# A cross-attention block on one core: pair 0's probabilities through the exchange instead of TensorE, two exchange targets by turns, x of batch two loaded later, row sums repeated by ACT

## The chip, the cores and the metric

The kernel runs on one core of one Trainium2 chip. A core has TensorE (PE, with its weight loads as PEld), VectorE (DVE), ScalarE (ACT), GpSimd (POOL) and SyncE (SP), each working through its own instructions in order and waiting for the others by semaphores. Sixteen DMA engines move data; here nearly all transfers are issued by SP, in order. The metric is the time of one execution on the device in microseconds; less is better.

## The reference, cut to what matters

Four batches, 512 rows of x and 512 of the encoder each, width 512, 16 heads of 32, an MLP of 2048. All float32; the mask is all ones.

```
x = layer_norm(hidden_states, ln1_w, ln1_b)
q = (x @ q_w + q_b)            # heads of 32
k = (encoder @ k_w + k_b)
v = (encoder @ v_w + v_b)
scores = einsum('bhqd,bhkd->bhqk', q, k) / sqrt(32)
attn = softmax(where(mask, scores, min))
out = einsum('bhqk,bhkd->bhqd', attn, v) @ cproj_w + cproj_b
hidden = out + hidden_states
y = layer_norm(hidden, ln2_w, ln2_b)
y = gelu(y @ fc_w + fc_b) @ proj_w + proj_b
return hidden + y
```

## The kernel before

**Units.** The heads go in 16 groups w = 0 to 15, four heads of one batch each (batch w // 4). The 512 query rows of a group go in four tiles of 128, qt = 0 to 3. Unit u = 4w + qt is one (w, qt); two units of a group, qt = 0, 1 or 2, 3, make a half, and pair p = 2w + half numbers the halves from 0 to 31.

**One unit.** `scores` (L240 to L249): TensorE makes four score tiles of 128x512 into one PSUM tile `sc`, which is the only one, so that the next unit's scores wait until VectorE has read this one's. VectorE adds the mask and finds the row extreme (L245, one instruction and a short read for each head), ACT takes the exponential and adds up the rows (L249). `turn` (L277) then transposes each head's probabilities on VectorE in 32x32 blocks into `tb`. At the second unit of a pair it also makes the reciprocals of the row sums (L282), repeats each 32 times (`rr`, L284) and transposes that too (L285). `tb` has two buffers: a pair's transposes wait until the exchange of the pair two before it is through.

**The exchange.** 32x32 blocks transposed in place are not a transposed tile: the blocks must still change their places across partitions. `copies` (L319) does that by sixteen DMAs from SP, each from 32 partitions to 32 others, 136 KB each. Their target is `pT`, one buffer, for most pairs; `gt` for the pairs in `IN_G` = (2, 4, 6) (later the MLP's gelu results live there); `xe` for pairs 29 and 31. A pair that goes to `pT` is held back until the pair before it in `pT` has been used; `exchange` keeps that book (`waiting`, `held`).

**Pair 0** is the exception (`ON_PE`): `turn` transposes its 32 tiles of 128x128 on TensorE (`tpp`, L263), ACT and VectorE copy them out of PSUM (L268, L266), `over_sums` repeats the sums (L329) and `turn_sums` transposes them on TensorE (`tpr`, L337, L339). It has no exchange.

**Attend** (L362, L367): TensorE multiplies the transposed probabilities with the values `v`, VectorE scales with the repeated sums into `oT`. `AT` says at which unit pairs 1 to 6 are attended (pair 1 at u=7, 2 at 9, ..., 6 at 17); the others follow four units after their first unit, at even u. Attend stands ahead of the scores of its unit.

**What fills TensorE between.** `prep_k`, `prep_q`, `prep_v` make a group's k, q, v (`acck` L196, `accq` L206, `accv` L218; 3.5 to 3.8 us each), several groups ahead; each then loads the weights of the group two further on. `cproj` (`accc`, L399) follows a batch's last attend; LN2 and the MLP (`accf` L457, `accp` L467) of batches 0 and 1 fill the later groups. Batches 2 and 3 have their MLP at the end in seven half-size products (L561, L601). The results of all these go through one ring of four PSUM banks (`acc_tile`), each free again when VectorE or ACT has copied it out.

**Who sets the order.** Nothing is scheduled by a tool: the program order is written out, and each engine keeps it. `first[w]` and `later[w]` are lists of pieces of work with costs; `run` deals them out over the four units of a group, half a share before and half after the middle of each unit. `inputs(b)` gives four lists for batch b: x1 loads x, x2 is LN1 in three parts (statistics of two tiles, of two more with the reciprocal root on POOL, the normalisation), x3 transposes the result into `xT` (L137, L140, L142), x4 loads the encoder rows. `norm(0, ...)`, `stat(0, ...)` and `rs(0)` are LN2 of batch 0, `t2` its four transposes, `cb(0)` adds a bias on POOL.

Of the kernel before, what the change touches and what calls it, by code (L numbers as in the profile page):

```python
# [36 lines left out]
F32 = mybir.dt.float32  # L37
# [7 lines left out]
P = 128  # L45
B, L, D, H = 4, 512, 512, 16
HD = D // H
INNER = 4 * D
NT = L // P
ND = D // P  # L50
NG = ND
HG = H // NG
# [3 lines left out]
NI = P // HD  # L56
NW = B * NG
AHEAD = 3
NORMAL = 2
LAG = 4  # L60
IN_G = (2, 4, 6)
IN_XE = (29, 31)
AT = {7: 1, 9: 2, 11: 3, 13: 4, 15: 5, 17: 6}
ON_PE = (0,)
MW = 8
WARM = 9
PW = 2 * NT * HG * HD
# [7 lines left out]
def xattn_block(ctx: ExitStack, tc: tile.TileContext, x, encT, mask, q_w, k_w, v_w, c_w, fc_w, p_w, vecs, rows, out):  # L75
    nc = tc.nc
    scale = float(np.float32(1.0) / np.sqrt(HD).astype(np.float32))

    def pools(stack, **bufs):
        return [stack.enter_context(tc.tile_pool(name=n, bufs=k)) for n, k in bufs.items()]  # L80

    const, keep, hids, tiles, small = pools(ctx, const=1, keep=1, hids=6, tiles=4, small=4)
# [4 lines left out]
    one, two, kqp, five, six, fws = pools(att, one=1, two=2, kqp=4, five=5, six=6, fws=MW)  # L87
# [3 lines left out]
    ident = const.tile([P, P], F32, tag="ident", name="ident")  # L91
# [13 lines left out]
    S = {}  # L105
    Q = [nc.sync]

    def acc_tile(name):
        return ps_acc.tile([P, D], F32, tag="acc", name=name)
# [143 lines left out]
    def turn(w, qt):  # L253

        half, q = divmod(qt, 2)
        if 2 * w + half in ON_PE:
            if q == 0:

                S["pT", w, half] = two.tile([P, 2, NT, HG, P], F32, tag="tb", name=f"pT_{w}_{half}")
            for h in range(HG):  # L260
                tp = acc_tile(f"tpp_{w}_{qt}_{h}")
                for t in range(NT):
                    nc.tensor.transpose(tp[:, ts(t, P)], S["ps", w, qt][h][:, ts(t, P)], ident)  # L263
                o = S["pT", w, half][:, q, :, h, :]
                if h % 2:
                    nc.vector.tensor_copy(o, tp.rearrange("p (t q) -> p t q", t=NT))  # L266
                else:
                    nc.scalar.copy(o, tp.rearrange("p (t q) -> p t q", t=NT))  # L268
            return
        if q == 0:  # L270


            S["tb", w, half] = two.tile([P, NI, PW + 2 * HD], F32, tag="tb", name=f"tb_{w}_{half}")
        tb = S["tb", w, half]
        tv = tb[:, :, :PW].rearrange("p j (a t h q) -> p a h t j q", a=2, t=NT, h=HG)
        for h in range(HG):
            nc.vector.transpose(tv[:, q, h], S["ps", w, qt][h])  # L277
        if q == 0:
            return

        rs = small.tile([P, 2, HG], F32, tag="rsum", name=f"rsum_{w}_{half}")
        nc.vector.reciprocal(rs, S["sums", w][:, 2 * half : 2 * half + 2, :])  # L282
        rr = one.tile([P, 2, HG, HD], F32, tag="rr", name=f"rr_{w}_{half}")
        nc.vector.tensor_copy(rr, rs[:, :, :, None].broadcast_to([P, 2, HG, HD]))  # L284
        nc.vector.transpose(  # L285
            tb[:, :, PW:].rearrange("p j (a q) -> p a j q", a=2), rr.rearrange("p a h d -> p (a h d)")
        )
        waiting.append((w, half))
        if w < NW - 1 or half == 0:
            exchange()  # L290
# [3 lines left out]
    def exchange():  # L294

        while waiting:
            w, half = waiting[0]
            if 2 * w + half not in IN_G + IN_XE:
                if held:
# [5 lines left out]
    def copies(w, half):  # L305
        tb = S["tb", w, half]

        pair = 2 * w + half
        if pair in IN_G or pair in IN_XE:
            pT = (gt if pair in IN_G else xe).rearrange("p (i n) -> p i n", i=NI)  # L310
        else:
# [7 lines left out]
                q.dma_start(out=pT[ts(j, HD), i], in_=tb[ts(i, HD), j])  # L319
        S["pT", w, half] = pT  # L320

    def over_sums(w, half):

        if 2 * w + half not in ON_PE:
            return
        rs = small.tile([P, 2, HG], F32, tag="rsum", name=f"rsum_{w}_{half}")
        nc.vector.reciprocal(rs, S["sums", w][:, 2 * half : 2 * half + 2, :])
        rr = one.tile([P, 2, HG, HD], F32, tag="rr", name=f"rr_{w}_{half}")
        nc.vector.tensor_copy(rr, rs[:, :, :, None].broadcast_to([P, 2, HG, HD]))  # L329
        S["rr", w, half] = rr.rearrange("p a h d -> p (a h d)")  # L330

    def turn_sums(w, half):
        if 2 * w + half not in ON_PE:
            return
        tp = acc_tile(f"tpr_{w}_{half}")
        for q in range(2):
            nc.tensor.transpose(tp[:, ts(q, P)], S["rr", w, half][:, ts(q, P)], ident)  # L337
        rb = one.tile([P, 2 * P], F32, tag="rb", name=f"rb_{w}_{half}")
        nc.scalar.copy(rb, tp[:, : 2 * P])  # L339
        S["rb", w, half] = rb  # L340

    def attend(w, half):

        b, g = divmod(w, NG)
        if g == 0 and half == 0:
            S["oT", b] = one.tile([P, NG, L], F32, tag="oT", name=f"oT_{b}")
        v, pT = S["v", w], S["pT", w, half]
        on_pe = 2 * w + half in ON_PE
        av = acc_tile(f"av_{w}_{half}")
        o = S["oT", b][:, g, ts(half, 2 * P)]  # L350
        if on_pe:
            shape, kw = "p (a q) -> p a q", dict(a=2)
            p = [[pT[:, :, t, h, :] for h in range(HG)] for t in range(NT)]
            r = S["rb", w, half].rearrange(shape, **kw)
        else:
            shape, kw = "p (a i q) -> p a i q", dict(a=2, i=NI)
            pv = pT[:, :, :PW].rearrange("p i (a t h q) -> p t h a i q", a=2, t=NT, h=HG)
            p = [[pv[:, t, h] for h in range(HG)] for t in range(NT)]
            r = pT[:, :, PW:].rearrange("p i (a q) -> p a i q", a=2)
        for t in range(NT):  # L360
            for h in range(HG):
                nc.tensor.matmul(  # L362
                    av[ts(h, HD), : 2 * P].rearrange(shape, **kw), v[:, t, ts(h, HD)], p[t][h],
                    start=(t == 0), stop=(t == NT - 1),
                )
        o, a = o.rearrange(shape, **kw), av[:, : 2 * P].rearrange(shape, **kw)
        nc.vector.tensor_tensor(o, a, r, ALU.mult)  # L367
        if (w, half) in held:
            held.remove((w, half))
        exchange()  # L370
# [326 lines left out]
    def do(fn):  # L697
        return [(0.0, fn)]
# [66 lines left out]
    x1, x2, x3, x4 = inputs(1)  # L765
# [7 lines left out]
    first = [[] for _ in range(NW)]  # L773
    later = [[] for _ in range(NW)]
# [11 lines left out]
    def some(n):  # L786
        taken, mlp[:n] = mlp[:n], []
        return taken
# [7 lines left out]
    def cb(b):  # L796
        return do(lambda: c_bias(b))

    def pb_(b):
        return do(lambda: proj_bias(b))  # L800

    def rs(b):
        return do(lambda: ln_rs((2, b)))

    def stat(b, *ts_):
        return do(lambda: [stat2(b, t) for t in ts_])

    def norm(b, *ts_):
        return do(lambda: [norm2(b, t) for t in ts_])


    x1, x2, x3, x4 = inputs(2)
    first[3] = x1 + first[3] + cb(0)
    k, q, v = A(7)
    c, t2 = C(0), turns2(0)
    first[4] = [k] + x2[:1] + [q] + x2[1:2] + [v] + x4 + x2[2:]
    later[4] = c[:1] + x3[:2] + c[1:2] + x3[2:] + c[2:] + stat(0, 0, 1, 2, 3) + rs(0)
    k, q, v = A(8)
    first[5] = norm(0, 0, 1, 2, 3) + [q, k] + t2[:3] + [v] + t2[3:] + pb_(0) + some(5)
    k, q, v = A(9)  # L820
    x1, x2, x3, x4 = inputs(3)
    first[6] = [k, q] + some(5) + [v] + x1
    k, q, v = A(10)
    first[7] = [k, q] + x2[:1] + some(3) + x2[1:2] + some(3) + [v]

    k, q, v = A(11)
    first[8] = h_(1, 0, 1) + x2[2:] + [k, q] + x3[:2] + some(1) + x3[2:] + [v] + h_(1, 2, 3) + x4
    later[8] = cb(1) + C(1)
    k, q, v = A(12)
    first[9] = [q] + some(2) + [k] + some(3) + [v]  # L830
    k, q, v = A(13)
    first[10] = [k, q] + some(5) + [v]
    k, q, v = A(14)
    t2 = turns2(1)
# [3 lines left out]
    k, q, v = A(15)  # L838
# [6 lines left out]
    for w in range(NW):  # L845
        if w and w % NG == 0:
            make_mb(w // NG)
        work, rest = first[w], later[w]
        share = sum(c for c, _ in work + rest) / NT
        due = 0.0  # L850
        for qt in range(NT):
            u = w * NT + qt
            pair = AT.get(u, (u - LAG) // 2 if u >= LAG and u % 2 == 0 else None)
            if pair in AT.values() and u not in AT:
                pair = None
            if pair is not None:
                turn_sums(*divmod(pair, 2))
                attend(*divmod(pair, 2))
            scores(w, qt)
            on_pe = u // 2 in ON_PE  # L860
            if not on_pe:
                turn(w, qt)

            if qt == 2:
                work, rest = work + rest, []
            due += share / 2
            due -= run(work, due)
            if on_pe:
                turn(w, qt)
                if u % 2 == 1:  # L870
                    over_sums(w, qt // 2)
            due += share / 2
            due -= run(work, due)
        run(work + rest)
# [1 line left out]

    load_h(B - 1, *range(NT))
    run(some(2))
    turn_sums(NW - 1, 0)
    attend(NW - 1, 0)  # L880
    run(some(2))
    load_wa(0)
    run(some(2))
    turn_sums(NW - 1, 1)
    attend(NW - 1, 1)
    run(some(2))
    load_wa(1)
# [50 lines left out]
```

## Time and profile before

| | us |
|---|---|
| three runs | 825.77, 826.09, 826.44 |
| median of them | 826.09 |
| the profiled execution | 823.17 |
| its span, first to last instruction | 821.4 |
| TensorE busy | 805.0 |
| VectorE busy | 562.7 |
| ACT busy | 347.7 |
| POOL busy | 90.4 |
| exponentials on ACT (L249), 256 of 710 ns | 181.6 |
| block transposes on VectorE (L277), 248 of 690 ns | 161.6 |
| repeats of the sums on VectorE (L284), 31 of 414 ns | 12.8 |
| SP's waits for an attend's last step (L319 for L367), before 260 us | 25.3 |

The span is the part of an execution that the trace covers; all times in the trace count from its start. An engine's busy time is the sum over its instructions with overlaps counted once. Durations that a row gives for one instruction overlap with the next by some tens of ns: 690 ns for a transpose, but four of them start 0.60 us apart. In rows of waits the name behind the arrow is what ended the wait. The granted clock is TensorE's, as a share of full speed.

### The profile page before, as it was taken

What the parts mean: (1) busy time and instruction counts of PE and PEld (TensorE: products, weight loads), DVE (VectorE), ACT (ScalarE), POOL (GpSimd) and SP (SyncE); (2) the same over time, 40 slices, a digit from 0 to 9 for tenths busy, and PEclk for the clock granted to TensorE, in tenths of its full rate; (3) what the DMA queues carried; (4) which work ended last, traced back from release to release, by engine and by line L of the source; (5) the groups of instructions that cost most, each with busy time, mean ns of one, the idle gap of its engine ahead of it and who ended that gap; (6) DMA issues with size and microseconds to landing.
All of it is one profiled execution on the core that took longest, in us unless ns stands there. A gap on an engine that the chain in (4) does not pass through costs nothing.

```text
span 821.4 us, 11900 instructions
## 1 busy us (share of the span) xinstructions
PE 805.0 (98%) x4020; PEld 467.0 (57%) x4020; DVE 562.7 (69%) x1264; ACT 347.7 (42%) x741; POOL 90.4 (11%) x98
## 2 busy tenths in 40 slices
PE   9998999999999999999999999999999999999998
PEld 6553545454454554454544444434447888888887
DVE  3598989886576778667886667787426986268511
ACT  2455555346554744365435367556201331023200
POOL 1110003112000111000111210010201012200011
PEclk9998999999999999999999999999999999999999
DMA  9639998856668768677676676777734550023001
GB/s 327 231 88 237 239 247 233 218 147 161 173 164 222 183 166 237 162 209 194 159 212 179 157 197 159 199 181 174 211 116 162 193 171 14 26 77 89 2 13 39
DMA packets 59740, 134.91 MB, mean 164 GB/s; under 512 B 12144, under 2 KB 14320, under 8 KB 59552
## 3 DMA queue, kind: packets, MB, share of 16 engines
q1 hardware_dynamic: 58416, 130.73, 58.8%
q0 software_dynamic: 736, 2.29, 0.8%
q10 hardware_dynamic: 528, 1.14, 0.5%
q8 instruction: 32, 0.52, 0.3%
q14 instruction: 28, 0.23, 0.1%
HBM read 58.74 MB, written 6.29 MB: 79 GB/s over the span
## 4 chain that ended last, share of the span: by engine, by line
PE 85%; DMA 5%; DVE 5%; SPq 3%; issue 1%; ACT 1%; DVEq 0%; ACTq 0%
PE accp L467 14%; PE accf L457 14%; PE q L561 12%; PE sc L240 7%; PE accc L399 7%; PE av L362 6%; PE accv L218 4%; PE acck L196 4%; PE accq L206 4%; SPq L319 3%; PE q4p L601 2%; PE q3p L601 2%; PE q7p L601 2%; PE q2p L601 2%; PE q5p L601 2%; PE q6p L601 2%
## 5 line engine op out<-in xcount | busy, mean ns | idle before, releaser
L249 ACT ACTIVATE s<-s,mn 128x512 f32<-128x512 f32 x256 | 181.6, 710 | 138.0 <-DVE mn L245 137.8
L245 DVE CUSTOM_DVE_ANT_0 s<-sc,mb 128x512 f32<-128x512 f32 x256 | 161.3, 686 | 55.4 <-PE sc L240 55.2
L277 DVE STREAM_TRANSPOSE tb<-s 128x512 f32<-128x512 f32 x248 | 161.6, 690 | 9.5 <-ACT s L249 8.5
L457 PE MATMUL accf<-yT,fcw 128*128 128x512 f32 x256 | 115.5, 599 | 0.5 <-ACT v L223 0.3
L467 PE MATMUL accp<-pw,gt 128*128 128x512 f32 x256 | 115.0, 598 | 0.0
L457 PEld LDWEIGHTS accf<-yT,fcw 128*128 128x128 f32 x256 | 47.2, 190 | 65.5 <-issue 55.5
L467 PEld LDWEIGHTS accp<-pw,gt 128*128 128x128 f32 x256 | 47.2, 190 | 63.8 <-issue 61.1
L240 PE MATMUL sc<-kT,qT 32*128 32x512 f32 x512 | 73.8, 646 | 1.1 <-ACT qT L209 0.8
L218 PEld LDWEIGHTS accv<-wv,xe 128*128 128x128 f32 x512 | 58.8, 192 | 9.9 <-issue 6.2
L218 PE MATMUL accv<-wv,xe 128*128 128x128 f32 x512 | 60.7, 277 | 1.7 <-ACT xe L142 0.9
L362 PE MATMUL av<-pT,v 128*32 128x256 f32 x864 | 53.9, 391 | 6.7 <-DMA pT<-tb 6.7
L561 PE MATMUL q<-ys,gt 128*128 128x256 f32 x256 | 60.1, 379 | 0.0
L196 PE MATMUL acck<-xe,wk 128*128 128x512 f32 x128 | 59.6, 609 | 0.0
L206 PE MATMUL accq<-xe,wq 128*128 128x512 f32 x128 | 58.5, 599 | 0.0
L399 PE MATMUL accc<-wc,oT 128*128 128x512 f32 x128 | 56.9, 597 | 0.0
L561 PEld LDWEIGHTS q<-ys,gt 128*128 128x128 f32 x256 | 48.6, 190 | 6.6
L249 ACT ACT_TABLE_LOAD x22 | 28.2, 1283 | 52.7 <-DVE mn L245 52.7
L230 POOL TENSOR_TENSOR v<-v,row 128x512 f32<-128x512 f32 x16 | 20.3, 1269 | 261.5 <-ACT v L223 261.4
L249 ACT ACTIVATION_READ_ACCUMULATOR s<-s,mn 128x1 f32 x256 | 47.7, 187 | 0.0
L362 PEld LDWEIGHTS av<-pT,v 128*32 128x32 f32 x864 | 26.1, 112 | 36.7 <-issue 18.9
L561 PE MATMUL q<-yT,gt 128*128 128x256 f32 x192 | 46.3, 379 | 0.0
L367 DVE TENSOR_TENSOR oT<-av,pT 128x256 f32<-128x256 f32 x26 | 11.0, 422 | 46.7 <-PE av L362 43.9
(117 smaller groups left out, 855.2 us busy)
## 6 DMA issues: line engine op xcount, KB each, us to landing
pT<-tb SPq DMA_DIRECT2D x416, 136.0 KB, 2.4
fcw<-fc_w_dram SPq DMA_DIRECT2D x32, 256.0 KB, 3.4
pw<-p_w_dram SPq DMA_DIRECT2D x32, 256.0 KB, 3.5
gt<-fc_w_dram SPq DMA_DIRECT2D x32, 256.0 KB, 3.0
gt<-tb SPq DMA_DIRECT2D x48, 136.0 KB, 2.8
wk<-k_w_dram SPq DMA_DIRECT2D x16, 256.0 KB, 3.5
xe<-encT_dram SPq DMA_DIRECT2D x16, 256.0 KB, 6.0
wv<-v_w_dram SPq DMA_DIRECT2D x16, 256.0 KB, 3.1
```

The lines of the kernel that those rows point to most:

```text
L196: nc.tensor.matmul(acc, S["wk", w][:, d, :], eT[:, d, :], start=(d == 0), stop=(d == ND - 1))
L218: nc.tensor.matmul(acc[:, ts(t, P)], eT[:, d, ts(t, P)], S["wv", w][:, d, :], start=(d == 0), stop=(d == ND - 1),)
L240: nc.tensor.matmul(sc[:, h, :], qT[r, ts(qt, P)], kT[r, :], start=True, stop=True)
L245: nc.vector.tensor_tensor_reduce(out=s, in0=sc[:, h, :], in1=S["mb", w // NG], scale=1.0, scalar=FMAX, op0=ALU.add, op1=ALU.min, accum_out=mn,
L249: nc.scalar.activation(s, s, AF.Exp, bias=mn, scale=-1.0, accum_out=sums[:, qt, h : h + 1])
L277: nc.vector.transpose(tv[:, q, h], S["ps", w, qt][h])
L362: nc.tensor.matmul(av[ts(h, HD), : 2 * P].rearrange(shape, **kw), v[:, t, ts(h, HD)], p[t][h], start=(t == 0), stop=(t == NT - 1),)
L399: nc.tensor.matmul(acc, S["oT", b][:, g, ts(t, P)], wc[:, g, :], start=(g == 0), stop=(g == NG - 1))
L457: nc.tensor.matmul(acc, S["fcw", b, f][:, d, :], S["yT", b][:, d, :], start=(d == 0), stop=(d == ND - 1))
L467: nc.tensor.matmul(acc, gT[q % 2][:, k, ts(t, P)], S["pw", b, q * FQ + k], start=(k == 0), stop=(k == FQ - 1))
L561: nc.tensor.matmul(o, a[:, k], y[:, k], start=(k == 0), stop=(k == 1))
L601: nc.tensor.matmul(o[:, t], a[:, c, ts(t, P)], w[:, c], start=(c == 0), stop=(c == NP - 1))
```

## The change

It has four parts, all in how the work is ordered and on which engine it stands.

1. Pair 0 is treated as the others: its eight score tiles are transposed by VectorE and go through an exchange, and it is attended at u=5 in place of u=4. `ON_PE`, `over_sums` and `turn_sums` go.
2. `IN_G` becomes (1, 3, 5, 7): in batch zero `pT` and `gt` take the pairs by turns.
3. x of batch two is loaded by the first piece of w=4 (it was the first of w=3), behind the exchanges of batch zero; its statistics and normalisation move among the `cproj` pieces of w=4, its transposes to w=5, and the order of the pieces of w=5 changes with them.
4. In `turn`, for every pair, `rr` is made by ACT. At the second unit of a pair VectorE transposes three heads, then takes the reciprocals, then transposes the fourth head while ACT repeats the sums.

```diff
-IN_G = (2, 4, 6)
+IN_G = (1, 3, 5, 7)
 IN_XE = (29, 31)
-AT = {7: 1, 9: 2, 11: 3, 13: 4, 15: 5, 17: 6}
-ON_PE = (0,)
+AT = {5: 0, 7: 1, 9: 2, 11: 3, 13: 4, 15: 5, 17: 6}
...
     def turn(w, qt):
         half, q = divmod(qt, 2)
-        if 2 * w + half in ON_PE:
-            if q == 0:
-                S["pT", w, half] = two.tile([P, 2, NT, HG, P], F32, tag="tb", name=f"pT_{w}_{half}")
-            for h in range(HG):
-                tp = acc_tile(f"tpp_{w}_{qt}_{h}")
-                for t in range(NT):
-                    nc.tensor.transpose(tp[:, ts(t, P)], S["ps", w, qt][h][:, ts(t, P)], ident)
-                o = S["pT", w, half][:, q, :, h, :]
-                if h % 2:
-                    nc.vector.tensor_copy(o, tp.rearrange("p (t q) -> p t q", t=NT))
-                else:
-                    nc.scalar.copy(o, tp.rearrange("p (t q) -> p t q", t=NT))
-            return
...
-        for h in range(HG):
+        for h in range(HG - q):
             nc.vector.transpose(tv[:, q, h], S["ps", w, qt][h])
         if q == 0:
             return
         rs = small.tile([P, 2, HG], F32, tag="rsum", name=f"rsum_{w}_{half}")
         nc.vector.reciprocal(rs, S["sums", w][:, 2 * half : 2 * half + 2, :])
         rr = one.tile([P, 2, HG, HD], F32, tag="rr", name=f"rr_{w}_{half}")
-        nc.vector.tensor_copy(rr, rs[:, :, :, None].broadcast_to([P, 2, HG, HD]))
+        nc.scalar.copy(rr, rs[:, :, :, None].broadcast_to([P, 2, HG, HD]))
+        nc.vector.transpose(tv[:, q, HG - 1], S["ps", w, qt][HG - 1])
         nc.vector.transpose(
             tb[:, :, PW:].rearrange("p j (a q) -> p a j q", a=2), rr.rearrange("p a h d -> p (a h d)")
         )
...
     x1, x2, x3, x4 = inputs(2)
-    first[3] = x1 + first[3] + cb(0)
+    first[3] += cb(0)
     k, q, v = A(7)
     c, t2 = C(0), turns2(0)
-    first[4] = [k] + x2[:1] + [q] + x2[1:2] + [v] + x4 + x2[2:]
-    later[4] = c[:1] + x3[:2] + c[1:2] + x3[2:] + c[2:] + stat(0, 0, 1, 2, 3) + rs(0)
+    first[4] = x1 + [k, q, v] + x4
+    later[4] = c[:1] + x2[:1] + c[1:2] + x2[1:2] + c[2:3] + x2[2:] + c[3:] + stat(0, 0, 1, 2, 3) + rs(0)
     k, q, v = A(8)
-    first[5] = norm(0, 0, 1, 2, 3) + [q, k] + t2[:3] + [v] + t2[3:] + pb_(0) + some(5)
+    first[5] = x3[:2] + [k] + x3[2:] + norm(0, 0, 1, 2, 3) + [v] + t2[:2] + [q] + t2[2:] + pb_(0) + some(5)
...
```

In the order that results, the instructions of each engine differ in these places: TensorE loses the 34 transposes of pair 0, attends it behind the values chain of w=3, and has the transposes of x of batch two (`tp_2_0` to `tp_2_3`) among `acck` and `accv` of w=8; on SP exchange 0 stands ahead of wq of w=3 and wk of w=4 and w=5, x of batch two behind exchange 7, and exchange 8 ahead of the encoder rows of batch two; on POOL a value bias of w=7 stands ahead of the reciprocal root of batch two's LN1; on ACT every pair's second unit has the repeat behind its exponentials.

## The prediction

> **What bounds the kernel now.** I write u = 4w + qt for the unit of scores (w, qt), pair p for units 2p and 2p+1, and "exchange p" for the sixteen copies of pair p. The page's first part comes first: it says which engine is the bound.
>
> ```profile
> PE 805.0 (98%) x4020; PEld 467.0 (57%) x4020; DVE 562.7 (69%) x1264; ACT 347.7 (42%) x741; POOL 90.4 (11%) x98
> ```
>
> TensorE idles 16 us in all, so time comes from those idles, from work taken off it, or from waits added. Next, busy time by stage, with borders at the events below: stretch, length, busy time of PE, PEld, DVE, ACT, POOL, granted clock, DMA share, GB/s.
>
> ```profile
> 20.00:42.00 22.00, 20.55 (x110) 11.78 (x109) 11.51 (x31) 10.43 (x24) 4.49 (x5) 1.00 0.62 229
> 42.00:54.70 12.70, 12.70 (x102) 7.90 (x102) 12.56 (x32) 7.17 (x19) 1.27 (x1) 1.00 0.11 36
> 54.70:82.40 27.70, 23.55 (x124) 11.09 (x123) 24.92 (x66) 16.79 (x44) 1.27 (x1) 0.88 0.88 225
> 82.40:141.90 59.50, 59.50 (x420) 32.71 (x420) 55.30 (x134) 33.60 (x86) 9.48 (x8) 1.00 0.92 240
> 141.90:190.30 48.40, 44.14 (x258) 21.98 (x257) 38.98 (x91) 19.06 (x43) 9.85 (x10) 1.00 0.65 169
> 190.30:821.40 631.10, 625.89 (x2932) 368.13 (x2928) 412.46 (x899) 256.01 (x522) 62.08 (x64) 1.00 0.56 149
> ```
>
> The DMA engines stand almost idle from 42 to 54.7 (0.11) and are then full to 142; VectorE has 0.14 us of slack in 42 to 54.7. So early on PE's 100% hides a chain VectorE -> exchange -> attend. The order of time on TensorE (start, length, work, idle before it) shows where that surfaces:
>
> ```profile
> 27.58 1.91 PE L263 MATMUL tpp<-ident,s 128*128 128x128 f32 x16
> 34.02 1.89 PE L263 MATMUL tpp<-ident,s 128*128 128x128 f32 x12
> 36.54 0.66 PE L263 MATMUL tpp<-ident,s 128*128 128x128 f32 x4 [0.62 <-ACT qT L209]
> 50.08 0.38 PE L337 MATMUL tpr<-ident,rr 128*128 128x128 f32 x2
> ...
> 66.78 3.64 PE L362 MATMUL av<-pT,v 128*32 128x256 f32 x32 [3.34 <-DMA pT<-tb]
> 82.39 1.93 PE L362 MATMUL av<-gt,v 128*32 128x256 f32 x32 [0.45 <-DMA gt<-tb]
> 145.31 1.93 PE L362 MATMUL av<-pT,v 128*32 128x256 f32 x32 [3.40 <-DMA pT<-tb]
> ```
>
> and SP's queue what the exchanges stand behind:
>
> ```profile
> 54.68 10.12 SPq L319 DMA_DIRECT2D pT<-tb  x16
> 68.22 12.27 SPq L319 DMA_DIRECT2D gt<-tb  x16
> ...
> 115.28 1.87 SPq L155 DMA_DIRECT2D xn<-x_dram  x4
> 117.73 13.28 SPq L319 DMA_DIRECT2D gt<-tb  x16
> 132.72 10.29 SPq L319 DMA_DIRECT2D pT<-tb  x16
> ```
>
> An exchange costs SP 10.1 us and lands 2.4 us later (median of L319); right behind 1 to 1.5 MB of loads it takes 12.3 to 13.3.
>
> **Step 1, transposes off TensorE.** Next start less start, 1.84 + 3.01 + 0.32 = 5.2 us of PE go (the 0.62 wait included). That is not the gain: PE then waits for attend 1, so the path is VectorE's. Its order: x of batch one lands at 30.60 (both kernels), then stats to 32.24. New chain: scores of u=1 2.45 (four starts 0.61 apart) -> 34.7; three transposes at 0.60 -> 36.5; reciprocal 0.2; last transpose 0.6; transpose of the sums 0.4 -> 37.7; two stats 1.6; u=2 scores and transposes 2.45 + 2.41 -> 44.2; four norms 1.8 -> 46.0; u=3 2.45 + 1.8 + 0.2 + 0.6 + 0.4 -> 51.4. Before, pair 1 was ready at 54.6, because VectorE waited for tpp (2.1 + 0.5 + 1.3) and for scores behind them (1.9). So exchange 1 can start 3.2 us sooner although VectorE transposes eight tiles more.
>
> **Step 2, the added exchange.** Exchange 0: 37.8 to 47.9, landed 50.3; attend 0 at u=5 needs it at about 53 (sc of u=4 at 48.4 waits for VectorE, then a values chain, 3.7). Hidden by the idle queue; without that cover it would cost its 10 us. But wq, wk and wk (three 256 KB loads, issued at 34 and 41 to 46 before) now stand behind it and ahead of exchange 1. They delay it by 0 (drained by 51.4) to 3.3 us (0.79 MB at 240 GB/s); they go out from 48 on, so I take 0.5. Exchange 1 starts 2.8 us sooner. From it to attend 2 SP's order is unchanged, so attend 2 starts at 82.4 - 2.8 = 79.6. PE idles about 2 us at u=4, 3.6 before attend 1 and 2 to 3 before attend 2; these contain the removed work.
>
> The row first: after the 3.34 us idle the clock was 0.50 from 66 to 72 us, after the 3.40 us idle at 142 it stayed 1.00. The Trainium skill, "TensorE: Matmul & The Clock Gate" (section "Why this matters for your kernels"), warns of idles above about 3 us between bursts; the second idle shows that one need not halve the clock. By the rule attend 1 and the next scores would again take 3.64 and 1.96 instead of 1.93 and 1.14, 2.5 us more; by the row 0 or 2.5. Either way they end before exchange 2 lands, so the sum doesn't move.
>
> **Step 3, buffers by turns, x moved.** Pairs 1, 3, 5, 7 take gt and 0, 2, 4, 6 pT: the same alternation with the parity swapped, nothing by itself, except that pair 7 leaves pT free for pair 8. From 82.4 to 141.9 PE ran without a wait; the same instructions, from 79.6, end at 139.1. Exchange 6 no longer stands behind x: 117.7 - 2.8 - 2.0 = 113.0, plus 10.3, plus 1.6 for three weights -> 124.9. Pair 7 is ready at 126 (u=15's scores 2.8 sooner, and a repeat of 0.82 us less on VectorE): 126 + 10.1 + 2.4 = 138.5, under 139.1. The 3.40 wait goes; attend 7 starts at 139.1 instead of 145.3: **6.2 us ahead**. Margin 0.6.
>
> **Step 4, what x meets behind.** x's four loads (1.9 us of SP, some 5.4 to land) now stand ahead of wk, wq and exchange 8; they land near 144, wanted near 147. Encoder rows of batch two are moved behind exchange 8: issued 152 to 154, landed at 159.5, wanted at 161. What does cost is VectorE: from sc of u=18 (3 us after attend 7) it has u=18 4.9, u=19 5.4, four h adds 2.4, x's stats 3.2 and norms 1.9, LN2 stats 3.2, oT 0.4, so u=20's scores begin 24.4 us after attend 7, though PE offers them at 20. ACT's xe copy of tp_2_0 stands behind u=20's exponentials, kT behind that; tp_2_3 and the values chain need their two banks and wait 2.5 to 3. Counted by PE's pieces, the first accf begins 43.0 us after attend 7. Before: 190.3 (end of sc u=22) - 145.3, less accf 0's 3.6, = 41.4, including waits of 1.6. So **1.6 us is given back** (bounds: 1.6 gained if nothing waits, 4 lost if ACT and VectorE miss each other once more).
>
> **Step 5, sums repeated by ACT.** 31 copies (414 ns mean, 293 undisturbed) leave VectorE. No row has this copy on ACT; bounds are 0.29 (VectorE's own) and 1.30 (its longest); I take 0.36, ACT's copy of 128x256 at L339. The last transpose (0.60) covers it; at 1.30 each pair would be ready 0.7 us later. But ACT now waits for the reciprocal with its evictions queued behind: at 371.5 scores end, three transposes and reciprocal end near 373.5, ACT was free at 372.7, so 1.1 us later; with a table load behind, 0.55. After 190 nothing waits on VectorE, so its gain is nothing; ACT's delay is hidden by the four banks (accf ends at 354.2, its gelu at 357.8, its bank is next wanted after three more chains, near 364). PE waited for ACT only twice there, 0.87 each; 0 to 1, I take 0.2.
>
> **Sum.** 6.2 - 1.6 - 0.2 = 4.4 us. The profiled execution took 823.17 (span 821.4 and 1.8 around it), so 818.8; the shown runs have median 826.09, 2.9 above, and I carry the difference over: **821.7**.
>
> A rule that speaks against the change is in the Trainium skill, "VectorE: DVE Perf Modes" (section "Rules for kernel authors"): a 128x128 transpose goes to TensorE where its result may land in PSUM. By the rule, moving these off TensorE buys an exchange of 10 us for nothing, and the sum would be 831.7; by the row of stage 42.00:54.70 (DMA share 0.11) that exchange runs in an empty queue and costs 0, which is what I take.
>
> **Rivals.**
> - *Larger gain.* No wait in step 4, exchange 1 undelayed: 6.7 + 1.6 = 8.3, 817.8. For it: those 2.5 us hang on one ACT order; against it: VectorE's sum. Chance 0.20.
> - *Nothing comes of it.* The three loads delay exchange 1 by 3.3 rather than 0.5 and pair 7's margin is lost: 4.4 - 2.8 - 1 is about 0.6, 825.5. Speaks for it: 12.3 us of exchange 2 behind loads. Against: 3.5 us between their issue and pair 1's readiness. 0.13.
> - *Slower: ACT's wait reaches PE.* 24 pairs after 190 us, 0.55 to 1.1 each, some 20 us on ACT, with the gelu and value copies behind. From 30% of it on PE (6 us) the change is slower; at 45%, 9 us, the time is 830.7. For it: every odd unit has it, and PE there has 100% to lose. Against: six us of bank slack at 357. 0.21.
> - *The forecast*, 819.5 to 824.4: 0.46.
>
> Measurements of this kernel can't tell less than about 0.2% (1.65 us) from no change. Faster: 0.46 + 0.20 = 0.66; same 0.13; slower 0.21. The range of 8 in 10 leaves 0.05 below 818.0 and 0.14 of the slower case above 828.0.
>
> **What would show it.** Step 1: reciprocal of pair 1 near 50.3. Step 2: exchange 1 issued near 52, PE waiting there and before attend 2 near 79.6. Step 3: no wait at attend 7, near 139. Step 4: a wait of 2 to 3 us before the values chain of w=8 near 165. Step 5: PE as full after 190 as before. I am wrong if exchange 1 starts after 54, or if ACT waits appear on PE past 190 us.

## The result, and the profile after

| | before | after |
|---|---|---|
| median, us | 825.77 (824.24 to 826.44, five runs) | 820.96 (818.40 to 823.18, five runs) |
| profiled execution, us | 823.17 | 818.40 |
| its span, us | 821.4 | 816.6 |
| its mean granted clock | 0.996 | 0.998 |

The ratio is 0.9944, with an interval of [0.9921, 0.9966]: 4.8 us faster, both in the medians and in the two profiled executions. The first part of the page of after (busy time, share of the span, instructions):

```profile
PE 798.2 (98%) x3986; PEld 462.9 (57%) x3986; DVE 546.8 (67%) x1237; ACT 354.6 (43%) x766; POOL 90.5 (11%) x98
```

TensorE is busy 6.8 us less (mostly the 34 transposes, and some time at a halved clock) with the same share of the span, so it idles 18 us, 2 more than before. Busy time of after by stage, with borders at its own events (exchange 1 issued, attend 2, attend 7, first `accf`); columns as before:

```profile
50.67:78.83 28.16, 24.10 (x153) 11.49 (x153) 24.07 (x64) 18.35 (x47) 2.55 (x2) 0.94 0.90 231
...
138.86:182.41 43.55, 39.93 (x249) 20.30 (x248) 38.35 (x92) 18.14 (x44) 9.88 (x10) 1.00 0.69 186
182.41:816.60 634.19, 629.16 (x2940) 369.61 (x2936) 402.19 (x878) 263.13 (x543) 62.21 (x64) 1.00 0.56 149
```

The stretch from exchange 1 to attend 2 takes 28.2 us as it did before (27.7): it has moved as a whole, and TensorE still has 4 us of idle in it. The order of time on TensorE in after (start, length, work, idle before it):

```profile
47.98 1.14 PE L239 MATMUL sc<-kT,qT 32*128 32x512 f32 x8 [1.82 <-DVE mn L244]
...
62.97 2.55 PE L322 MATMUL av<-gt,v 128*32 128x256 f32 x32 [2.44 <-DMA gt<-tb]
65.45 2.09 PE L239 MATMUL sc<-kT,qT 32*128 32x512 f32 x8
...
78.83 1.93 PE L322 MATMUL av<-pT,v 128*32 128x256 f32 x32 [1.62 <-DMA pT<-tb]
...
138.86 1.93 PE L322 MATMUL av<-gt,v 128*32 128x256 f32 x32
...
167.75 0.65 PE L136 MATMUL tp<-ident,xn 128*128 128x128 f32 x4 [2.86 <-ACT xe L141]
```

Attend 7 (138.86) has no wait ahead of it; the wait of 2.86 us at 167.75 is new. SP's queue in after:

```profile
37.22 10.10 SPq L305 DMA_DIRECT2D pT<-tb  x16
50.67 10.33 SPq L305 DMA_DIRECT2D gt<-tb  x16
...
64.12 12.80 SPq L305 DMA_DIRECT2D pT<-tb  x16
...
113.15 10.06 SPq L305 DMA_DIRECT2D pT<-tb  x16
125.82 10.26 SPq L305 DMA_DIRECT2D gt<-tb  x16
136.76 1.87 SPq L154 DMA_DIRECT2D xn<-x_dram  x4
```

Exchange 0 stands in the stretch where the queue was idle. Exchange 1 goes out 4.0 us sooner than before (0.5 of it because everything in this execution is that much earlier: the first scores of the kernel begin at 22.30 and 22.83). x of batch two now follows exchange 7, and exchange 6 takes 10.06 us instead of the 13.28 it took behind x.

The account at the events, after against before: attend 2 3.6 us sooner, attend 7 6.45 sooner. From attend 7 to the values chain that waits 0.87 us for an `xe` copy (299.57 before, 295.12 after), 2.0 are given back. From there to the end of the span after takes 521.5 and before 521.8: 0.3 are gained. 6.45 - 2.0 + 0.3 = 4.8. This account is that of two executions, and both are 2.6 us faster than the median of their kernel. A second profiled execution of the changed kernel (10 below) has attend 7 5.6 sooner, 3.6 given back, 1.7 of them at a halved clock, and the same 0.3: 2.3 in all. The 4.8 of the result rests on the medians.

### The profile page after: what moved, and what is told of

The parts are those of the page before. It is cut to its first block, busy times and chain, and to the rows that moved or that the text cites. A ratio compares the mean times of both kernels' runs of the same rounds, so it can differ in the third digit from the quotient of the medians.

```text
span 816.6 us, 11880 instructions
## 1 busy us (share of the span) xinstructions
PE 798.2 (98%) x3986; PEld 462.9 (57%) x3986; DVE 546.8 (67%) x1237; ACT 354.6 (43%) x766; POOL 90.5 (11%) x98
## 4 chain that ended last, share of the span: by engine, by line
PE 84%; DVE 7%; DMA 5%; SPq 2%; ACT 1%; issue 1%; DVEq 0%; ACTq 0%
PE accf L417 14%; PE accp L427 13%; PE q L521 12%; PE sc L239 7%; PE av L322 7%; PE accv L217 5%; PE accc L359 5%; PE accq L205 4%; PE acck L195 4%; DVE s L244 3%; DVE tb L262 2%; SPq L305 2%; DMA xn<-x_dram 2%; PE q4p L561 2%; PE q3p L561 2%; PE q7p L561 2%
## 5 line engine op out<-in xcount | busy, mean ns | idle before, releaser
L262 DVE STREAM_TRANSPOSE tb<-s 128x512 f32<-128x512 f32 x224 | 146.3, 691 | 12.3 <-ACT s L248 9.5
L521 PEld LDWEIGHTS q<-ys,gt 128*128 128x128 f32 x256 | 48.6, 190 | 6.6
L322 PE MATMUL av<-pT,v 128*32 128x256 f32 x832 | 50.3, 382 | 2.1 <-DMA pT<-tb 1.6
L525 ACT ACTIVATE ga<-uc,vec 128x256 f32<-128x256 f32 x32 | 16.3, 508 | 60.1 <-DVE uc L493 60.1
```

Of the source, the lines that this page charges most:

```text
L322: nc.tensor.matmul(av[ts(h, HD), : 2 * P].rearrange(shape, **kw), v[:, t, ts(h, HD)], p[t][h], start=(t == 0), stop=(t == NT - 1),)
L521: nc.tensor.matmul(o, a[:, k], y[:, k], start=(k == 0), stop=(k == 1))
```

## The experiments

Twelve runs follow. Ratios are to the kernel before, run beside them on the same chip. The starts are those of the profiled executions. The first scores, ahead of which the kernels are alike, begin anywhere from 21.89 to 22.98 us, so that half a microsecond in a start says nothing.

| kernel | exchange 1 | attend 2 | attend 7 | wait ahead of it | span | median | ratio [95%] |
|---|---|---|---|---|---|---|---|
| before | 54.68 | 82.39 | 145.31 | 3.40 | 821.4 | 825.77 | |
| after | 50.67 | 78.83 | 138.86 | 0 | 816.6 | 820.96 | 0.9944 [0.9921, 0.9966] |
| 1 idle transposes added | 52.10 | 79.25 | 139.74 | 0.64 | 817.5 | 821.51 | 0.9956 [0.9939, 0.9972] |
| 2 sums on VectorE | 51.96 | 80.15 | 141.13 | 0.55 | 821.4 | 823.33 | 0.9968 [0.9949, 0.9987] |
| 3 x early | 50.80 | 79.28 | 143.20 | 2.75 | 820.3 | 822.88 | 0.9966 [0.9948, 0.9984] |
| 4 pair 1 to pT | 55.98 | 83.30 | 142.86 | 0 | 822.4 | 824.33 | 0.9991 [0.9975, 1.0007] |
| 5 LN2 later | 51.10 | 78.87 | 141.00 | 0.98 | 823.5 | 825.26 | 1.0002 [0.9988, 1.0017] |
| 6 LN1 later | 47.36 | 81.10 | 141.74 | 1.12 | 821.1 | 821.66 | 0.9962 [0.9947, 0.9977] |
| 7 both later | 46.69 | 79.98 | 140.55 | 1.06 | 822.5 | 823.47 | 0.9983 [0.9972, 0.9993] |
| 8 before, sums on ACT | 53.50 | 81.63 | 145.72 | 4.44 | 823.4 | 824.94 | 0.9990 [0.9976, 1.0004] |
| 9 waits filled | 51.08 | 79.38 | 140.47 | 0.53 | 819.9 | 820.86 | 0.9937 [0.9917, 0.9957] |
| 10 after again | 50.54 | 78.10 | 139.69 | 1.47 | 819.1 | 821.68 | 0.9949 [0.9933, 0.9965] |
| 11 before, waits filled | 54.37 | 83.06 | 147.01 | 0.81 | 823.1 | 824.25 | 0.9982 [0.9967, 0.9998] |
| 12 targets alone | 52.40 | 81.68 | 145.61 | 2.81 | 823.4 | 824.31 | 0.9986 [0.9969, 1.0002] |

The name behind an arrow is that of the event that came last by the profile, and at attend 7 it misleads in some rows. In every execution with a wait there, attend 7 starts 0.2 to 0.35 us after the last copy of exchange 7 has landed, also in 1, 2, 9 and 10, whose rows name ACT, and in 8, whose row names a load: all these waits are for exchange 7. In after that copy landed at 138.65, 0.2 us ahead of attend 7, so even there nothing was to spare.

**1. Is it TensorE's work?** After, with as many transposes put back as were taken away, at the places where pair 0's were, writing a tile that nobody reads.

```diff
+        if w == 0 and half == 0:
+            idle = acc_tile(f"idle_{qt}")
+            for i in range(4 * NT):
+                nc.tensor.transpose(idle[:, ts(i % NT, P)], ident, ident)
```

> The changed kernel with TensorE work added back: 32 transposes of the identity, 16 behind the scores of each of the first two units, where pair 0's stood, read by nobody. My theory: attend 1 and attend 2 wait for exchanges, which hang on VectorE, so the 3.7 us of TensorE work disappear into those waits but for some 0.5 us (the scores of u=2 come that much after VectorE wants them): attend 2 at 79.3 in place of 78.8, time 0.3 to 0.8 us above the changed kernel. Rival: TensorE is 98% busy, so work taken off it is time: 3.7 us slower than the changed kernel, attend 2 near 82.5.

821.51 us, 0.55 above after; span 0.9 longer. The waits ahead of u=3, u=4 and attend 2 shrink from 1.20, 1.82 and 1.62 us to 0, 0.92 and 0.55: 3.2 of the 3.9 us of transposes disappear in them. Attend 7 comes at 139.74, where the two executions of after have 138.86 and 139.69. What left TensorE is therefore not what was won.

**2. The row sums back on VectorE** (part 4 undone).

```diff
-        for h in range(HG - q):
+        for h in range(HG):
...
-        nc.scalar.copy(rr, rs[:, :, :, None].broadcast_to([P, 2, HG, HD]))
-        nc.vector.transpose(tv[:, q, HG - 1], S["ps", w, qt][HG - 1])
+        nc.vector.tensor_copy(rr, rs[:, :, :, None].broadcast_to([P, 2, HG, HD]))
```

> The changed kernel with its fourth part undone: the row sums are repeated by VectorE behind all four transposes. My theory: exchanges 0 and 1 are ready 0.3 and 0.7 us later (0.33 us of VectorE for each pair, more where POOL works beside it), the chain to attend 2 shifts by as much, past 190 us nothing changes: 0.5 to 1.5 us slower than the changed kernel. Rival (ACT's wait for the reciprocals reaches TensorE past 190 us): the time falls below the changed kernel's by some of the 0.5 to 1.1 us for each of 24 pairs.

823.33 us, 2.4 above after: the direction of the theory, and more of it. Exchange 1 starts 1.3 us later, attend 7 2.3 later. TensorE in this kernel:

```profile
141.13 1.93 PE L321 MATMUL av<-gt,v 128*32 128x256 f32 x32 [0.55 <-ACT s L248]
...
170.51 1.12 PE L136 MATMUL tp<-ident,xn 128*128 128x128 f32 x4 [3.35 <-ACT xe L141]
```

The wait near 168 is 3.35 instead of 2.86, and the transposes behind it take 1.12 instead of 0.65: the granted clock was 0.50 from 170 to 176, which after's profiled execution didn't have at that place. So of the 4.8 us that its span is longer 2.3 are there by attend 7 and 2.5 come behind it, with the clock. Against 10, which lost clock at that place too, attend 7 is 1.4 later and the span 2.3 longer; the medians say 2.4 in all.

**3. x of batch two back ahead of exchange 6** (part 3 undone).

```diff
-    first[3] += cb(0)
+    first[3] = x1 + first[3] + cb(0)
...
-    first[4] = x1 + [k, q, v] + x4
-    later[4] = c[:1] + x2[:1] + c[1:2] + x2[1:2] + c[2:3] + x2[2:] + c[3:] + stat(0, 0, 1, 2, 3) + rs(0)
+    first[4] = [k] + x2[:1] + [q] + x2[1:2] + [v] + x4 + x2[2:]
+    later[4] = c[:1] + x3[:2] + c[1:2] + x3[2:] + c[2:] + stat(0, 0, 1, 2, 3) + rs(0)
...
-    first[5] = x3[:2] + [k] + x3[2:] + norm(0, 0, 1, 2, 3) + [v] + t2[:2] + [q] + t2[2:] + pb_(0) + some(5)
+    first[5] = norm(0, 0, 1, 2, 3) + [q, k] + t2[:3] + [v] + t2[3:] + pb_(0) + some(5)
```

> The changed kernel with its third part undone: x of batch two is loaded by the first piece of w=3 and normalised and transposed in w=4 as before. My theory: exchange 6 gets 12 to 13 us again instead of 10.1, exchange 7 is issued some 3 us later, attend 7 waits about 3 us; in return the 2.9 us wait for ACT near 165 goes: 0 to 1.5 us slower than the changed kernel. Rival (moving x is what brings the gain): 3 us or more slower. Rival (moving x costs): faster by 1 us or more.

822.88 us, 1.9 above after, a little over what was expected. Attend 7 on TensorE, and x and exchanges 6 and 7 on SP:

```profile
143.20 2.79 PE L322 MATMUL av<-gt,v 128*32 128x256 f32 x32 [2.75 <-DMA gt<-tb]
```

```profile
113.56 1.88 SPq L154 DMA_DIRECT2D xn<-x_dram  x4
...
116.02 11.92 SPq L305 DMA_DIRECT2D pT<-tb  x16
...
129.96 10.87 SPq L305 DMA_DIRECT2D gt<-tb  x16
```

The wait is back, attend 7 is 4.3 us later (3.5 later than in 10), and the wait near 168 is gone: 4.3 lost there and 2.9 of it saved behind it, as the steps had it.

**4. Pair 1 to `pT`, behind attend 0** (part 2 undone).

```diff
-IN_G = (1, 3, 5, 7)
+IN_G = (2, 4, 6)
```

> The changed kernel with IN_G = (2, 4, 6) again: pairs 0 and 1 both go to pT, so exchange 1 is held until attend 0 has run at u=5. My theory: exchange 1 starts near 55.8 instead of 50.7 and behind 1.5 MB of loads, attend 1 at 69 to 71, attend 2 at 84 to 86 instead of 78.8, and with it all that follows: 5 to 7 us slower than the changed kernel, about the kernel before or slower. Rival (targets don't matter since SP issues one exchange after the other anyway): within 1 us of the changed kernel.

824.33 us, 3.4 above after: same as before. TensorE at attend 1:

```profile
68.09 3.64 PE L322 MATMUL av<-pT,v 128*32 128x256 f32 x32 [7.39 <-DMA pT<-tb]
```

Exchange 1 must wait for attend 0 to free `pT`, goes out at 55.98 behind two weights and the encoder rows, and the wait triples. By attend 7 4.0 us are left of the 5.3 lost at exchange 1. Without the second target, exchange 0 gives nothing. The edit also sends pair 7 to `pT`, so that exchange 8 goes out behind attend 7, at 147.29 instead of 140.63; attend 8 then waits 0.34 us, so this side of the edit costs little.

**5, 6, 7. Can the waits that are left be taken away?** In 5 LN2's statistics go behind the scores of u=20, to free VectorE and ACT ahead of the wait near 168. In 6 LN1 of batch one goes from w=0 to w=1, off VectorE's chain to pair 1. 7 is both. Edits of 5 and 6:

```diff
-    later[4] = c[:1] + x2[:1] + c[1:2] + x2[1:2] + c[2:3] + x2[2:] + c[3:] + stat(0, 0, 1, 2, 3) + rs(0)
+    later[4] = c[:1] + x2[:1] + c[1:2] + x2[1:2] + c[2:3] + x2[2:] + c[3:]
...
-    first[5] = x3[:2] + [k] + x3[2:] + norm(0, 0, 1, 2, 3) + [v] + t2[:2] + [q] + t2[2:] + pb_(0) + some(5)
+    first[5] = x3[:2] + [k] + x3[2:] + stat(0, 0, 1, 2, 3) + rs(0) + norm(0, 0, 1, 2, 3) + [v, q] + t2 + pb_(0) + some(5)
```

```diff
-    first[0] = [(CHAIN, lambda: prep_v(1))] + x2[:1] + [(CHAIN, lambda: prep_q(1))] + x2[1:2] + [k2] + x2[2:] + [k3, v2]
-    first[1] = [(CHAIN, lambda: (prep_v(3), load_enc(1)))] + [q2, q3] + x3[:2]
+    first[0] = [(CHAIN, lambda: prep_v(1)), (CHAIN, lambda: prep_q(1)), k2, k3, v2]
+    first[1] = [(CHAIN, lambda: (prep_v(3), load_enc(1)))] + x2[:1] + [q2] + x2[1:] + [q3] + x3[:2]
```

> The changed kernel with LN2's statistics of batch zero moved from the end of w=4 to w=5, behind the transposes of u=20, and q of w=8 put ahead of LN2's four transposes. My theory (step 4: the wait near 165 is VectorE's list of work ahead of the scores of u=20, passed on by ACT's order): the scores of u=20 start 3.2 us sooner, at 160 instead of 163.3, the 2.9 us wait at the transposes of x goes, and some 1.5 us come back as a wait for LN2's transposed rows ahead of the first accf: 1 to 3 us faster than the changed kernel. Rival (the wait is the transposes' own banks, or x's arrival): the wait stays and the time is within 0.5 us of the changed kernel's.

> The changed kernel with LN1 of batch one (its x lands at 30.3 us and VectorE waits for it between the first two units) moved from w=0 to w=1. My theory (the first 79 us hang on VectorE's order ahead of exchanges 0 and 1): the scores of u=1 no longer wait for x, exchange 0 is issued near 34 instead of 37.2 and exchange 1 near 46 to 47 instead of 50.7, attend 2 comes at 75 to 76 instead of 78.8, and half or more of that is kept to the end: 2 to 4 us faster than the changed kernel. Rival (the exchanges are bound by SP and the DMA engines from 55 us on, whatever VectorE does first): attend 2 at 78 or later and less than 1 us gained.

> Both edits, LN1 of batch one in w=1 and LN2's statistics of batch zero in w=5. If the two waits are independent, the gains add: 3 to 7 us faster than the changed kernel, 814 to 818 in the median. If the second only passes on what the first saves, no more than the better of the two.

All three missed: 825.26, 821.66 and 823.47, 4.3, 0.7 and 2.5 above after. In 5 the wait near 168 did go, and this stands in its place on TensorE:

```profile
183.33 1.12 PE L136 MATMUL tp<-ident,xn 128*128 128x128 f32 x4 [4.15 <-ACT qT L208]
```

It comes from VectorE (start, length, work, idle before it):

```profile
173.16 4.75 DVE L127 TENSOR_SCALAR xn<-h,mv,rs 128x512 f32<-128x512 f32 x4 [1.41 <-POOL rs L123]
177.84 0.68 DVE L244 CUSTOM_DVE_ANT_0 s<-sc,mb 128x512 f32<-128x512 f32 x1
```

TensorE's scores of u=21 are done at 172.3. VectorE waits 1.41 us for POOL's reciprocal root, norms for 4.75 and reads them only at 177.84; ACT's exponentials end at 181.5, the `qT` copy stands behind them, and the bank that TensorE needs stands behind that. The clock was then 0.50 from 181 to 188. In 6 the same piece does the same thing earlier:

```profile
59.67 1.93 PE L322 MATMUL av<-gt,v 128*32 128x256 f32 x32 [1.63 <-DMA gt<-tb]
...
72.93 2.09 PE L239 MATMUL sc<-kT,qT 32*128 32x512 f32 x8 [2.00 <-DVE mn L244]
...
81.10 1.93 PE L322 MATMUL av<-pT,v 128*32 128x256 f32 x32
```

Attend 1 comes 3.3 us sooner, as expected. Then VectorE waits 1.45 us for POOL and norms, the transposes of x wait 1.31 and the scores 2.00, the clock is 0.50 from 72 to 79, and attend 2 has no wait any more but stands 2.3 later than in after. The rival of 6 had the numbers right and not the reason: exchange 2 landed at 74.52, and TensorE's own delay set attend 2. So LN1 in w=0 is not free, but it is cheaper there than in w=1, where TensorE soon wants its result; both waits were moved, not removed.

**8. Part 4 alone, in the kernel before.** The edit is that of 2, the other way round.

> The kernel before with the fourth part alone: ACT repeats the row sums of pairs 1 to 31, the rest as it was. My theory after the run that put the sums back on VectorE: VectorE is the slow link up to 140 us in the kernel before too, exchange 1 starts some 0.6 us sooner, attend 7 comes 0.5 to 1.5 us sooner, past 190 us nothing: 0.5 to 2 us faster than the kernel before. Rival (ACT's wait for the reciprocals costs TensorE past 190 us): slower than the kernel before. Rival (the fourth part is the change): 4 us or more faster.

824.94 against 825.39 beside it, an interval that reaches over 1: at most 2 us, most likely less than 1. Exchange 1 starts 1.2 us sooner and exchange 7, behind x and exchange 6 as in before, 1.3 sooner (131.39). But attend 7 waits 4.44 instead of 3.40 and is no sooner: the last copy of exchange 7 took 4.4 us from issue to landing, where before's took 2.5. What held it isn't shown.

**9, 10, 11. Are the waits worth their length, or the clock behind them?** Several waits above are followed by a halved clock. 9 is after, and 11 before, with idle transposes in the waits; 10 is after itself. 9, whose `av` is overwritten by attend's own products (11 has 24 each for attend 1 and 7):

```diff
+        for i in range({1: 18, 2: 12}.get(2 * w + half, 0)):
+            nc.tensor.transpose(av[:, ts(i % NT, P)], ident, ident)
         for t in range(NT):
```

> The changed kernel with 18 and 12 identity transposes written into the target of attend 1 and of attend 2 ahead of their own matmuls, which overwrite them. They hang on nothing, so they lie in the waits of 2.44 and 1.62 us ahead of those two; by 0.123 us each (1.97 us for 16 in the run with 32 idle transposes) they fill 2.2 and 1.5 us of them. Theory: an idle PE is what halves the granted clock afterwards (0.50 from 64 to 68 after the wait of 2.44 us, 1.7 us lost), so with the waits filled the clock stays 1.00 from 60 to 100 and attend 2 starts within 0.5 us of 78.83; the time is 0.5 to 2.5 us below the changed kernel run beside it. Rival A: the clock drops for another reason (the moment, or the transfers that are running), so the drop near 64 stays and the time is the same within 0.7. Rival B: the extra work makes attend 1 and 2 late in most executions, 0.5 to 1.5 us slower.

> The changed kernel itself, unaltered, beside the two others on the same chip: a second profiled execution of the same instructions. Theory: the waits stand where they stood, within 0.5 us each (2.4 ahead of attend 1, 1.6 ahead of attend 2, 2.9 near 167), and the places where the granted clock halves differ from the first profile; what the execution is longer than 818.4 us is what the clock lost, within 0.7 us. Median 820 to 822. Rival: the spread of 818.4 to 823.2 comes from waits that move, and the clock loses about 1.8 us in every execution.

> The kernel before with 24 identity transposes each ahead of attend 1 and attend 7, written into their targets and overwritten: 2.95 us by 0.123 each, in waits of 3.34 and 3.40 us. Theory: the wait itself remains but the clock no longer halves after it (0.50 from 65 to 72 in the profile of before, 3.4 us lost), so 1.5 to 3.5 us faster than before. If that is so, part of the 4.8 us of the change is the clock's. Rival: the idle time isn't what halves the clock, and the time is that of before within 0.7 us.

9 took 820.86, 10 took 821.68, and their ranges lie over each other, so the time is not settled. TensorE in 9:

```profile
60.87 2.19 PE L321 MATMUL av<-ident 128*128 128x128 f32 x18
63.30 1.93 PE L324 MATMUL av<-gt,v 128*32 128x256 f32 x32 [0.24 <-issue]
...
75.78 1.47 PE L321 MATMUL av<-ident 128*128 128x128 f32 x12
79.38 1.93 PE L324 MATMUL av<-pT,v 128*32 128x256 f32 x32 [2.12 <-DMA pT<-tb]
```

The clock stayed 1.00 through this stretch, where after, 10, 1 and 2 had lost 1.7 us behind a wait of 2.4 to 3.4 us ahead of attend 1, so idling is what had halved it. But attend 2 gained nothing: the time that TensorE saved stands as a longer wait, 1.47 filled and 2.12 idle instead of 1.62. From exchange 1 to attend 2 it is 28.3 us here and 28.2 in after, and attend 2 starts 0.14 us after the last copy of exchange 2 has landed: exchange 2 sets this start, not TensorE. In 11 the clock was 1.00 from the start to the end of TensorE's work, where before had lost 3.4 us. Its attends:

```profile
67.64 1.93 PE L364 MATMUL av<-pT,v 128*32 128x256 f32 x32 [1.75 <-DMA pT<-tb]
...
83.06 1.93 PE L364 MATMUL av<-gt,v 128*32 128x256 f32 x32 [2.77 <-DMA gt<-tb]
...
147.01 1.93 PE L364 MATMUL av<-pT,v 128*32 128x256 f32 x32 [0.81 <-DMA pT<-tb]
```

All three wait for their exchange; exchange 1 took 11.36 us in this execution, 10.12 in before. Over all executions the mean granted clock is 0.9991 in 11 and 0.9944 in before beside it, 3.9 us less lost. The time gained is 0.0018 in the ratio, 1.5 us with an interval from 0.2 to 2.7, and 2.3 us in the medians: the low end of the theory. So a part of the clock that is lost ahead of a late exchange, here about half, is lost in a wait that would be there anyway. In the change itself the clock has a small share: 0.9953 in 10 against 0.9944 in before beside it, 0.7 us.

10 shows what the spread of after is made of. Granted clock of after (third column from the right) from 168 to 173:

```profile
168.00:173.00 5.00, 5.00 (x44) 4.12 (x42) 3.48 (x7) 1.63 (x3) 0.09 (x1) 1.00 0.83 190
```

and of 10:

```profile
168.00:173.00 5.00, 4.42 (x23) 4.26 (x24) 4.31 (x8) 1.88 (x3) 0.00 (x0) 0.66 0.74 169
```

The wait ahead was 2.86 us in both. 10's execution is 2.5 us longer: 1.7 of it is the clock here, where no transfer is awaited, and 0.8 an attend 7 that is later by a wait of 1.47. That wait is new against what was expected of 10, and it is exchange 7's, which took 10.26 us in after and 11.72 here and landed at 139.50:

```profile
125.11 11.72 SPq L305 DMA_DIRECT2D gt<-tb  x16
```

```profile
139.69 1.93 PE L322 MATMUL av<-gt,v 128*32 128x256 f32 x32 [1.47 <-ACT rr L269]
```

The `rr` of the row is pair 8's and has no part in attend 7.

**12. Parts 1 and 2 alone**, that is after with the edits of 2 and 3 together.

> Parts 1 and 2 of the change alone: no probabilities transposed on TensorE and the two targets by turns, while x of batch two is loaded where it was (part 3 undone) and the row sums are repeated by VectorE (part 4 undone). Theory: exchange 1 starts near 52 and attend 2 near 80, 2 to 3 us sooner than in before, but exchange 6 again stands behind x of batch two (116 in the run with part 3 undone) and, with the sums on VectorE, attend 7 falls to 144 to 145.5, with a wait of 2 to 3.5 us ahead of it, against 145.3 in before: nearly all of the sooner start is given back there, and the time is 0 to 1.5 us below before. Undoing parts 3 and 4 cost 1.9 and 2.4 us by themselves; adding the two gives 0.5 us below before. Rival: the sooner start is kept through 145 to 190 whatever x does, and the time is 2 to 3.5 us below before.

824.31 us, 1.7 below the 826.02 beside it by medians, and 0.0014 with an interval that includes no change: the theory's 0 to 1.5, give or take. TensorE at attends 1, 2 and 7:

```profile
64.72 3.19 PE L321 MATMUL av<-gt,v 128*32 128x256 f32 x32 [3.29 <-DMA gt<-tb]
...
81.68 3.24 PE L321 MATMUL av<-pT,v 128*32 128x256 f32 x32 [3.06 <-DMA pT<-tb]
...
145.61 3.49 PE L321 MATMUL av<-gt,v 128*32 128x256 f32 x32 [2.81 <-DMA gt<-tb]
```

and its exchanges 2 and 6 on SP:

```profile
65.85 13.91 SPq L304 DMA_DIRECT2D pT<-tb  x16
...
119.64 11.70 SPq L304 DMA_DIRECT2D pT<-tb  x16
```

Exchange 1 starts 2.3 us sooner than in before; exchange 2, behind the encoder rows, takes 13.9 and leaves 0.7 of it; behind x nothing is left at attend 7 (145.61 against 145.31).

**What each part is worth.** The ratio falls from 1 to 0.9986 with parts 1 and 2, by another 0.0018 with part 3 (run 2) or 0.0020 with part 4 (run 3), and to 0.9944 or 0.9949 with both (runs of after). In microseconds (times 826): about 1.2, 1.5 to 2, 1.5 to 2. Each of these has an uncertainty of about its own size; that parts 3 and 4 together bring more than half of the whole is the likely reading, not a proven one. Attend 7's start points the same way: 145.31 in before, 145.61 with parts 1 and 2, 143.20 with part 4 added, 141.13 with part 3 added, 138.86 and 139.69 with all.

## Why the prediction was right

**Step 1** (transposes are not the gain; VectorE's chain is). The first half is shown by run 1, the second by runs 2 and 6, where VectorE's list moves exchange 1 by 1.3 us later and 3.3 sooner. Pair 1 was ready at 50.6 (forecast 51.4); the waits at u=4, attend 1 and attend 2 were 1.8, 2.4 and 1.6, where 2, 3.6 and 2 to 3 were forecast.

**Step 2.** Exchange 0 ran from 37.22 (37.8) and attend 0 never waited for it. The three loads behind it delayed exchange 1 by nothing: it went out at 50.67, when pair 1 was ready at 50.64; 0.5 was taken. Attend 2 came at 78.83 (79.6). The clock did halve after the wait ahead of attend 1, for 3.4 us, and as the step said the sum did not move: run 9 shows it.

**Step 3.** Attend 7 at 138.86 (139.1), without a wait, and exchange 6 at 113.15 (113.0), in 10.06 us. The margin of 0.6 us was smaller than the step had it, because the landing of exchange 7 was taken at the median of 2.4 us and took 3.2: the last copy landed at 138.65. That there was no wait in the profile is luck: 10 had 1.47, and 1, 2, 5, 6, 7 and 9, with x behind exchange 7 and two targets too, 0.5 to 1.1. That most of the 3.40 went is not. Run 12 shows what the step didn't spell out: this is where the whole sooner start is kept or lost. It also corrects one clause, "From it to attend 2 SP's order is unchanged, so attend 2 starts at 82.4 - 2.8": the order doesn't fix the time. Exchange 2 took 12.27 in before, 12.80 in after and 13.91 in 12, and in 12 only 0.7 of 2.3 us arrived.

**Step 4.** The wait near 165 came as described, for the xe copy behind ACT's exponentials: 2.86 (2.5 to 3). The first `accf` begins 43.55 us after attend 7 (43.0). Given back were 2.0, not 1.6, and 3.6 in 10, where the clock halved behind this wait. Run 5, with another order of the same pieces, took 48.28 from attend 7 to the first `accf`, 4.7 more than after: the step was right to set a bound of 4 lost for a worse meeting of ACT and VectorE.

**Step 5** was right that ACT's wait reaches nothing behind 190. ACT's repeat took 0.40 us (0.36 taken) and waited 0.6 us a pair for the reciprocals (0.55 to 1.1), and from 295 us on 0.3 were gained where 0.2 lost were forecast, a difference too small to read. Waits on TensorE behind 190 are 0.9 and 0.7 us, where before had 0.9 and 0.9. The rival that made ACT's wait the loss would have shown on TensorE there, and it doesn't. What the step hides is how much part 4 is worth as a part: its sooner pair 1 had been booked under steps 1 and 3, so that it looked like a cost. Run 2 puts it at 2.4 us by the medians and 1.6 to 2 by the ratios, a third or more of the result.

**Sum.** 6.45 - 2.0 + 0.3 = 4.8 against 6.2 - 1.6 - 0.2 = 4.4. The terms came out one by one, so the match is more than luck, but its closeness is luck: the same account of 10, against the same execution of before, gives 2.3. The carry of 2.9 us from the profiled execution to the median fitted as well; the medians of the two sets of runs are 820.96 and 821.68, the forecast 821.7. Of the rivals, "larger gain" needed the wait of step 4 to stay away, and it came. "Nothing comes of it" had 3.3 us of delay for exchange 1, which was 0; its time is near that of parts 1 and 2 alone, for another reason. The rule of the Trainium skill, "VectorE: DVE Perf Modes" (section "Rules for kernel authors"), sends 128x128 transposes to TensorE. The 10 us that the prediction put on going against it were not paid: attend 0 didn't wait for its exchange, nor did exchange 1.

## What to carry to other kernels

Where a chain of transfers sets the pace, as here up to 140 us, work off TensorE (3.9 us put back cost 0.55), a sooner start (2.3 us left nothing at attend 7 in run 12) and even a halved clock (3.9 us regained brought about 2) are worth less than their length; follow the gain through every transfer behind it to the last consumer that waits, because one load ahead of one exchange can take all of it back. A part that only shortens an engine's list by a microsecond can be worth a third of the whole, if that list feeds the chain; price it by undoing it, not by where its instructions go. And a wait that is filled by moving work, as in 5 and 6, is only gone if the moved work isn't wanted soon behind its new place.

## What the runs showed of the hardware that was not expected

*The clock is lost in equal pieces, on a fixed grid.* The granted clock was 1.00 or 0.50 and nothing between, and what one low stretch inside TensorE's work costs (the sum of 1 - clock) was 1.7 us, 3.4 us or 5.1 us, in all profiled executions: 1.71 after the 2.44 us wait in after, 3.41 after the 3.34 us wait in before, 5.12 around the 7.39 us wait in run 4. The length of a single idle doesn't decide it: the 1.82 us that end near 48 were followed by a low stretch in run 5 (0.50 from 48.6 to 52.0) and by none in after, 9 and 10, and the 3.40 us at 142 in before by none either.

What decides is how the idle lies on a grid. Cut each execution into pieces of 3.41 us from the start of a low stretch, forwards and backwards: every other low stretch of it starts and ends on a border too. In run 5 the 1.82 us lie within one piece, 45.17 to 48.58; in after a border at 47.08 parts them into 0.9 and 0.9. In before a border at 143.72 parts the 3.40 us into 1.8 and 1.6. Over all profiled executions, from 20 us on, the clock was low behind each of the 31 pieces with more than 2.03 us of idle in them, behind 7 of the 17 with 1.67 to 2.03, and no low stretch began behind one with less. The Trainium skill, "TensorE: Matmul & The Clock Gate" (section "What's actually happening"), has a window of about 3.4 us that runs freely; the grid agrees with that. Its idle of one whole window (~3.4 us) before the clock halves does not agree: here 60% of one was enough every time.

*An exchange is not 10 us.* The sixteen copies took 10.0 to 10.4 us in half of the cases and up to 13.9 behind loads. Twice they took 11.4 in a queue in which nothing had gone out for 8 us (exchange 0 in run 1, exchange 1 in 11). The same exchange of the same kernel differed by 1.5 us between two executions (exchange 7: 10.26 in after, 11.72 in 10; exchange 8: 11.50 and 12.97). The last copy landed 2.4 us after its issue in most cases, but that of exchange 7 took 3.2 in after and 4.4 in 8. With 0.2 us to spare at attend 7, this decides whether the wait there appears.
